# The second half of the swap of the fifth and sixth pairs' inverses: issued by ScalarE in place of SyncE

## The chip, the cores and the metric

The kernel runs on one core of a Trainium2 chip. The metric is the device time of one execution in microseconds; before the change the median of 3 runs is 2953.59 us (2952.55 to 2953.98).

## What is computed

The reference takes 64 graphs of 256 nodes with 512 features each, and one adjacency matrix for all of them. It has two layers, each with a residual and a layer normalisation:

```
# layer 0
mi, mj = x @ Wi.T, x @ Wj.T
x = layernorm(x + deg * (mi + b) + adj @ mj)
# layer 1: attention of 8 heads of 64 channels, masked by the adjacency
q, k, v = x @ Wq.T + bq, x @ Wk.T + bk, x @ Wv.T + bv
attn = softmax(where(adj == 0, -inf, q @ k.T / 8))
x = layernorm(x + (attn @ v) @ Wo.T + bo)
```

The part of interest is the division of the softmax: the products of the exponentials with v are divided by the sums of the exponentials.

## The kernel before

**Groups.** The 64 graphs are worked on in 32 groups of two. A loop (`for g in range(NG - 1)`) runs over the first 31; in one round it does the attention of group g and the first layer of group g + 1. The last group's attention stands behind the loop. All tensors are float32. Most matrix products are made from three parts of each operand (a head rounded down to the fast format, a low part and a "diff"), so each operand of a product is cut by three instructions on three engines: the head by ScalarE, the diff by VectorE (L683), the low part by GpSimd or VectorE (L686).

**Order.** Nearly every instruction is issued through `in_order`, so each engine and each engine's DMA queue runs its instructions as they stand in the code: an instruction that waits holds up all that comes after it on that engine. SyncE does nothing but issue DMAs; ScalarE issues some between its activations.

**Pairs and their division.** The 8 heads of a graph are 4 pairs; the two graphs of a group have 8 pairs, w = 0 to 7 in the code. `scores(g, w)` makes the scores of a pair and returns a step that makes the exponentials: the mask is added by VectorE (L910), the exponential taken by ScalarE (L914), and GpSimd adds two halves (L924). `values(g, w)` multiplies with v into the PSUM tile pav. After each second pair `divide_two` copies pav to the tile aoT (ScalarE, L958) and calls `divide`. That one sums the exponentials on TensorE (den), and its inner step `end` takes the reciprocal on VectorE (L1009) into the first half of the tile spread. The other half of spread gets the same numbers with the two halves of the partitions exchanged: this is the swap, two DMAs from SBUF to SBUF of 64 KB each (L1012). ScalarE sums the inverses for a check (L966). Later `multiply` multiplies aoT by spread on GpSimd (L952), which needs both halves of the swap.

For the last two pairs of a group (w = 7, `last`) the second half of the swap is issued by ScalarE and the sum comes later. For the fifth and sixth pairs (w = 5) `divide_two` is called with `apart=True`, and returns the step `end` so that the loop can place it: it is called `invert` there.

**The loop around the change** (parts left out). The step `invert` stands between the values of the seventh and the eighth pair (L1222); the first line makes the exponentials of the eighth:

```
        later()
        second.neighbours()
        values(g, 6)
        invert()
        fetch_h(b1, 1)
        values(g, 7)
...
        first.give(0)
        multiply()
        second.add(1)
        send_h(b1, 0)
        total_up = divide_two(g, 7)
        split_head(*ao_parts(g, 1, upper))
        go_on()
        split_low(*ao_parts(g, 0, lower), nc.gpsimd)
        own()
        h11 = turn_h(b1, 1)
```

`send_h` (L702) writes rows of the normalised first layer to DRAM, `fetch_h` (L707) reads them back in another order into the tile hB, and `turn_h` transposes hB on VectorE into hF (L517); all these DMAs are issued by SyncE. `give` normalises rows (ScalarE, L509 and L510). The head, low and diff parts of aoT lie in the tiles qT, v and kT at this point. `go_on` and `own` are products of these with Wo on TensorE.

Of the kernel before, what the change touches and what calls it, by code (L numbers as in the profile page):

```python
# [219 lines left out]
def unshifted_path(ctx, tc, flag, x, adj, wiT, wjT, b0, wqT, bq, wkT, bk, wvT, bv, woT, bo, out):  # L220
# [16 lines left out]
    nc = tc.nc  # L237
# [5 lines left out]
    NB = 2  # L243
    NG = B // NB
# [20 lines left out]
    def bank(name):  # L265
        return ps_m.tile([P, 512], F32, tag="mm", name=name)
# [11 lines left out]
    def in_order(ins):  # L278

        tc.keep_in_program_order(ins)  # L280
# [4 lines left out]
    def matmul(*args, **kw):  # L285
        in_order(nc.tensor.matmul(*args, **kw))  # L286
# [41 lines left out]
    rtot = const.tile([P, B, NC // 2], F32, name="rtot")  # L328
# [601 lines left out]
    def target(g, w):  # L930

        i, pr = divmod(w, NC)
        return aoT[g][:, pr // 2 * 2:pr // 2 * 2 + 2, i * N:(i + 1) * N]
# [20 lines left out]
    def divide_two(g, w, apart=False):  # L954

        dst = target(g, w)
        last = w == NB * NC - 1 and g < NG - 1
        in_order(nc.scalar.copy(dst, pavs[g]))  # L958
        i, pr = divmod(w, NC)
        end = divide(dst, [made.pop((g, w - 1))[1], made.pop((g, w))[1]],  # L960
                     rtot[:, NB * g + i, pr // 2:pr // 2 + 1], last, last or g == NG - 1 and w == 3)
        return end if apart else end()

    def total(rden, total_out):
        unused = p1.tile([P, N], F32, tag="unused", name="unused")
        in_order(nc.scalar.activation(unused, rden, AF.Identity, accum_out=total_out))  # L966
# [27 lines left out]
        low = p1.tile([P, 2, N], F32R, tag="xdiff" if g else "hD", name="early")  # L994
        return [both[:, 0], low, both[:, 1]], aoT[g][:, 0:2, :N]

    def divide(dst, pks, total_out, last, other):


        den = bank("den")[:, :N]  # L1000
        for pp in range(2):
            for j in range(2):
                q = 2 * pp + j
                matmul(den[q * R:(q + 1) * R, :], ones[:, :R], pks[pp][:, j, :], start=True, stop=True,
                       tile_position=(0, q * R))
        def end():
            spread = (p3 if other else p1).tile([P, 2, N], F32, tag="mj" if other else "spread", name="spread")
            rden = spread[:, 0, :]
            in_order(nc.vector.reciprocal(rden, den))  # L1009
            for half in range(2):  # L1010
                issuer = nc.scalar if last and half else nc.sync
                in_order(issuer.dma_start(out=spread[half * DH:(half + 1) * DH, 1, :],  # L1012
                                          in_=spread[(1 - half) * DH:(2 - half) * DH, 0, :]))
            products.append((dst, spread))
            if last:
                return lambda: total(rden, total_out)
            total(rden, total_out)

        return end
# [112 lines left out]
    for g in range(NG - 1):  # L1132
# [28 lines left out]
        values(g, 0)  # L1161
        values(g, 1)
        divide_two(g, 1)
        run([scores(g, 2), scores(g, 3)])
        load_xB(b3)
# [15 lines left out]
        early = cut_early(g)  # L1181
        split_head(*early)
        divide_two(g, 3)
        now, later = scores(g, 4), scores(g, 5)
        now()
# [21 lines left out]
        if g == 0:  # L1207
            add_output_bias(0)
            add_output_bias(1)
        first.stat(0)  # L1210
        invert = divide_two(g, 5, True)
        now, later = scores(g, 6), scores(g, 7)
        aoP[g] = three(("qT", "kT"))
# [88 lines left out]
    g = NG - 1  # L1302
# [18 lines left out]
    last = NB * NC - 1  # L1321
# [70 lines left out]
```

## Time and profile before

| | |
|---|---|
| median of 3 runs | 2953.59 us |
| profiled execution | 2951.97 us |
| its span, first to last instruction | 2950.1 us |
| TensorE matmul busy | 2878.1 us, 98% |
| VectorE busy | 2265.1 us, 77% |
| GpSimd busy | 1482.3 us, 50% |
| ScalarE busy | 1309.4 us, 44% |
| swap DMAs issued by SyncE | 223 |
| swap DMAs issued by ScalarE | 31 |
| mean granted TensorE clock | 0.999 |

The profile is of one execution. Lines such as L1012 are lines of the kernel; most matmuls are recorded under the line of one helper (L286) and told apart by their tiles. Names such as PE, DVE, ACT, POOL and SP stand for TensorE, VectorE, ScalarE, GpSimd and SyncE; a q behind the name (SPq) means the engine's sequencer, which issues DMAs. A timeline has the start in us from the span's beginning, the length, the instruction with its output and inputs, and in brackets the idle time ahead of it and what ended it. A wait list gives total us, times, and the longest. The chain that ended last is followed back from the last instruction, at each step to what released it. One round of the loop takes some 90 to 91 us.

### The profile page before, as it was taken

The numbers are of one execution on the slowest core, as the hardware profiler recorded it, in microseconds if no ns is written. First come the engines' busy times: TensorE is split into PE (matmuls) and PEld (weight loads), VectorE is DVE, ScalarE is ACT, GpSimd is POOL, SyncE is SP. The second block draws the span as 40 slices with busy tenths as digits, with TensorE's granted clock in tenths as the row PEclk, the third lists the DMA queues.
The fourth block names the chain that finished last, engine by engine and source line by source line (L and its number), as shares of the span: only waits on it lengthen the run. The fifth ranks groups of instructions, "written<-read, shape, count | busy, mean of one in ns | idle before, by whom it ended". The sixth has DMA issues, their size and how long they took to land.

```text
span 2950.1 us, 45509 instructions
## 1 busy us (share of the span) xinstructions
PE 2878.1 (98%) x16902; PEld 2140.1 (73%) x16902; DVE 2265.1 (77%) x3275; ACT 1309.4 (44%) x2412; POOL 1482.3 (50%) x1049
## 2 busy tenths in 40 slices
PE   9999999999999999999999999999999999999998
PEld 6577777777777777777777777777777777777775
DVE  5777787777877778877778777787777787777875
ACT  4444444444444444444444444444444444444443
POOL 3555555454555455454545544555545555454553
PEclk9999999999999999999999999999999999999999
DMA  7577766777666776667776677766677766777653
GB/s 251 194 258 239 247 218 218 255 245 266 217 219 239 266 247 230 212 226 264 242 247 222 221 249 252 268 212 215 238 267 240 246 214 215 257 248 261 213 211 116
DMA packets 303345, 690.54 MB, mean 234 GB/s; under 512 B 25744, under 2 KB 171280, under 8 KB 302864
## 3 DMA queue, kind: packets, MB, share of 16 engines
q1 hardware_dynamic: 282784, 588.02, 58.4%
q10 hardware_dynamic: 20336, 99.56, 9.5%
q8 instruction: 136, 2.23, 0.3%
q14 instruction: 89, 0.73, 0.1%
HBM read 589.04 MB, written 81.79 MB: 227 GB/s over the span
## 4 chain that ended last, share of the span: by engine, by line
PE 77%; DVE 15%; POOL 3%; DMA 3%; issue 1%; SPq 1%; ACT 1%; POOLq 0%; DVEq 0%; ACTq 0%
PE px L286 26%; PE pxy L286 20%; PE py L286 13%; PE ps L286 7%; PE pav L286 5%; PE pa L286 3%; DVE hF L517 2%; DMA hB<-h_cols 2%; DVE kT L683 2%; DVE spread L1009 2%; DVE st L496 2%; PE po L286 2%; DVE xh L833 1%; PE den L286 1%; DVE xh L830 1%
## 5 line engine op out<-in xcount | busy, mean ns | idle before, releaser
L924 POOL TENSOR_TENSOR pk<-pe 128x512 f32<-128x512 f32 x256 | 347.4, 1368 | 729.5 <-ACT pe L914 729.5
L914 ACT ACTIVATE pe<-pe 128x1024 f32<-128x1024 f32 x256 | 271.0, 1059 | 176.9 <-DVE pe L910 176.9
L504 POOL TENSOR_TENSOR rstd<-ve,mhalf 128x1 f32<-128x1 f32 x256 | 167.5, 654 | 343.4 <-DVE below L502 313.2
L910 DVE TENSOR_TENSOR pe<-ps,maskT 128x1024 f32<-128x1024 f32 x256 | 297.2, 1200 | 3.6 <-PE ps L286 3.6
L1009 DVE RECIPROCAL spread<-den 128x256 f32<-128x256 f32 x127 | 222.7, 1754 | 81.7 <-ACT aoT L958 51.8
L686 POOL TENSOR_TENSOR hL<-hF,hA 128x512 fp32r<-128x512 f32 x93 | 166.4, 1789 | 229.1 <-ACT hA L680 229.1
L774 DVE TENSOR_TENSOR kT<-py,kT 128x512 f32<-128x512 f32 x128 | 88.5, 692 | 226.2 <-ACT kT L773 226.2
L286 PE MATMUL ps<-qT,kT 64*128 64x256 f32 x2048 | 256.6, 390 | 0.0
L286 PE MATMUL pav<-pe,v_sb 128*32 128x256 f32 x4096 | 248.4, 382 | 3.5 <-DVE kT L774 1.5
L286 PEld LDWEIGHTS ps<-qT,kT 64*128 64x128 f32 x2048 | 187.3, 187 | 68.6 <-PE pav L286 26.3
L510 ACT ACTIVATE xh<-xh,shift,rstd 128x512 f32<-128x512 f32 x256 | 208.8, 816 | 8.6
L286 PEld LDWEIGHTS pav<-pe,v_sb 128*32 128x32 f32 x4096 | 120.0, 110 | 116.8 <-issue 24.4
L680 ACT ACTIVATE hA<-hF 128x512 fp32r<-128x512 f32 x124 | 78.3, 632 | 278.5 <-DVE hF L517 255.5
L286 PE MATMUL px<-factor,x_head 128*128 128x512 f32 x720 | 200.2, 400 | 0.0
L286 PE MATMUL py<-factor,x_diff 128*128 128x512 f32 x720 | 192.8, 390 | 2.0 <-ACT kT L773 2.0
L368 POOL TENSOR_TENSOR xh<-xh,degb 128x1024 f32<-128x1024 f32 x64 | 182.5, 2853 | 22.8 <-ACT degb L365 20.9
L286 PE MATMUL px<-factor,x_low 128*128 128x512 f32 x720 | 192.8, 390 | 0.0
L952 POOL TENSOR_TENSOR aoT<-aoT,spread 128x512 f32<-128x512 f32 x127 | 165.9, 1306 | 41.6 <-DMA spread<-spread 35.4
L686 POOL TENSOR_TENSOR x_low<-xT,x_head 128x1024 fp32r<-128x1024 f32 x60 | 144.2, 2403 | 67.6 <-ACT x_head L680 64.7
L286 PE MATMUL py<-hD,factor 128*128 128x512 f32 x640 | 175.9, 397 | 2.2 <-ACT kT L773 2.2
L286 PE MATMUL px<-hA,factor 128*128 128x512 f32 x640 | 175.7, 397 | 0.0
L496 DVE BATCH_NORM_STATS2 st<-xh 128x6 f32<-128x512 f32 x256 | 174.3, 681 | 0.2
(160 smaller groups left out, 6809.1 us busy)
## 6 DMA issues: line engine op xcount, KB each, us to landing
factor<-wi SPq DMA_DIRECT2D x120, 768.0 KB, 8.7
factor<-wo SPq DMA_DIRECT2D x120, 768.0 KB, 6.2
factor<-wv SPq DMA_DIRECT2D x93, 768.0 KB, 7.8
factor<-wk SPq DMA_DIRECT2D x93, 768.0 KB, 7.0
factor<-wq ACTq DMA_DIRECT2D x62, 768.0 KB, 7.6
factor<-wq SPq DMA_DIRECT2D x62, 768.0 KB, 7.4
xB<-in_x_dram SPq DMA_DIRECT2D x256, 128.0 KB, 4.1
xh<-in_x_dram SPq DMA_DIRECT2D x64, 512.0 KB, 3.9
```

The costliest lines, as they stand in the source:

```text
L286: in_order(nc.tensor.matmul(*args, **kw))
L368: in_order(nc.gpsimd.tensor_tensor(xh[b], xh[b], degb, ALU.add))
L496: order(nc.vector.bn_stats(st, t))
L504: order(nc.gpsimd.tensor_tensor(rstd, ve, mhalf, ALU.pow))
L510: order(nc.scalar.activation(t, t, AF.Identity, bias=shift, scale=rstd))
L686: in_order(engine.tensor_tensor(parts[1], src, parts[0].bitcast(F32), ALU.subtract))
L774: in_order(nc.vector.tensor_add(dst, Y, dst))
L910: in_order(nc.vector.tensor_add(pe.rearrange("p j t q -> p j (t q)"), ps.rearrange("p j t q -> p j (t q)"), maskT.rearrange("p t q -> p (t ...
L914: in_order(nc.scalar.activation(flat, flat, AF.Exp, scale=QSCALE, accum_out=etot[:, NB * g + i, pr:pr + 1]))
L924: in_order(nc.gpsimd.tensor_tensor(pk, pe[:, :, 0, :], pe[:, :, 1, :], ALU.add))
L952: in_order(nc.gpsimd.tensor_tensor(d, d, spread, ALU.mult))
L1009: in_order(nc.vector.reciprocal(rden, den))
```

## The change

The condition for ScalarE as issuer of the second half gets wider: beside the last pairs of a group in the loop it now takes every call with `apart=True`, which is the one for the fifth and sixth pairs (31 calls). `divide` gets this as a parameter of its own, `urgent`; what else hangs on `last` (where the sum is made, which pool spread comes from) stays as it is.

```diff
-                     rtot[:, NB * g + i, pr // 2:pr // 2 + 1], last, last or g == NG - 1 and w == 3)
+                     rtot[:, NB * g + i, pr // 2:pr // 2 + 1], last, last or g == NG - 1 and w == 3, last or apart)
...
-    def divide(dst, pks, total_out, last, other):
+    def divide(dst, pks, total_out, last, other, urgent):
...
             for half in range(2):
-                issuer = nc.scalar if last and half else nc.sync
+                issuer = nc.scalar if urgent and half else nc.sync
                 in_order(issuer.dma_start(out=spread[half * DH:(half + 1) * DH, 1, :],
                                           in_=spread[(1 - half) * DH:(2 - half) * DH, 0, :]))
```

## The prediction

> **What bounds the kernel now.** I read the first part of the page and the summary of the chain that ended last, then the chain itself across one group, then the timelines of the engines in the same 20 us, and last the list of waits.
>
> ```profile
> PE 2878.1 (98%) x16902; PEld 2140.1 (73%) x16902; DVE 2265.1 (77%) x3275; ACT 1309.4 (44%) x2412; POOL 1482.3 (50%) x1049
> PE 77%; DVE 15%; POOL 3%; DMA 3%; issue 1%; SPq 1%; ACT 1%; POOLq 0%; DVEq 0%; ACTq 0%
> ```
>
> TensorE is busy nearly throughout, yet the chain leaves it for a fifth of the span: VectorE, DMA and SyncE's queue hold pieces of the path. The chain in the group around 1316 us shows where:
>
> ```profile
> 1314.44 1.67 DVE spread L1009
> 1316.11 0.02 issue
> 1316.13 0.47 SPq L1012
> 1316.60 0.05 issue
> 1316.65 0.59 SPq L1012
> ...
> 1317.34 3.10 DMA hB<-h_cols
> 1320.43 0.02 issue
> 1320.46 1.13 DVE hF L517
> ...
> 1329.88 0.70 DVE xh L833
> 1330.59 0.04 issue
> 1330.63 0.97 PE pxy L286 x3
> ```
>
> Columns are start, length, what. The reciprocal of the fifth and sixth pairs (L1009) ends at 1316.11; SyncE issues both halves of the swap; only then can it issue the fetch of the turned h (hB, L707, at 1317.34); that lands at 1320.43 and VectorE transposes it into hF. From there VectorE works without a gap until TensorE is released at 1330.63. So the swap's second issue is on the path not for its data but because the fetch stands behind it in SyncE's queue.
>
> What else could hold VectorE at that point is its own next reciprocal, that of the seventh and eighth pairs:
>
> ```profile
> 1318.64 1.76 DVE L1009 RECIPROCAL spread<-den 128x256 f32<-128x256 f32 x1 [0.80 <-PE den L286]
> 1320.46 1.13 DVE L517 STREAM_TRANSPOSE hF<-hB 128x512 f32<-128x512 f32 x1
> ```
>
> It ends at 1320.40, only 0.06 before the transpose. In the timelines of the groups at 1679 and 2131 us, where the fetch came sooner, the transpose starts 4.21 us after the fifth and sixth pairs' reciprocal ended; that is the floor that the other reciprocal sets. I measured this start in groups 1 to 30 of the 31: mean 4.50, median 4.38, worst 5.58 us. From it to the next group's first reciprocal takes 59.25 us, within 0.1 us in 27 of the 29 groups where it can be measured, and from that first reciprocal to the fifth and sixth pairs' takes 26.75 us always. So every group's length follows that start one for one, down to 4.21.
>
> [...] for the seventh and eighth pairs both queues issue at 1320.43 (0.47 and 0.50 us), and over the run ScalarE's halves land 2.2 us after issue, SyncE's 2.1. [...] behind another swap the issue takes 0.59 instead of 0.47, the fetch right behind the swaps 0.53 against 0.35 for its line's median; the simultaneous pair shows no lengthening, but its ScalarE half lands 0.29 us later than SyncE's (1322.66 against 1322.37). [...] here swaps of 64 KB land 1.9 us or more after issue[...].
>
> **The change, part by part.** It touches 31 swaps, one in each group of the loop; the last group takes the other call and stays.
>
> 1. Removed from SyncE: one issue per group, 0.59 us and the 0.05 before it, 0.64 in all. The next in the queue is the fetch: 1317.34 becomes 1316.70. The fetch's data was sent at 1312.68 and is long there. [...] the fetch loses up to the 0.29 seen above. So the landing moves by 0.35 to 0.64 us; I take 0.5.
>
> 2. What this is worth. Each group gains the smaller of that shift and its distance from 4.21. The distances in the 30 groups are 1.37, 1.16, 0.67, 0.64, 0.50, 0.46, 0.45, 0.33, 0.32, 2 x 0.24, 2 x 0.23, 0.19, 2 x 0.17, 0.16, 2 x 0.15, 2 x 0.14, 0.11, 0.10, 0.09, 2 x 0.08, 0.05, 0.03, 2 x 0. Group 0, where the other reciprocal ends late, gains nothing. With a shift of 0.35 the sum is 5.9 us, with 0.5 it is 6.8, with 0.64 it is 7.4. More shift would bring little, because VectorE's reciprocal is late next.
>
> 3. Added to ScalarE: one issue, 0.50 us (the row of the other swap), in front of the sum of the inverses. It waits for the same reciprocal as that sum, so the wait is not new. Behind it stand these:
>
> ```profile
> 1316.14 0.42 ACT L966 ACTIVATE unused<-spread 128x256 f32<-128x256 f32 x1
> ...
> 1316.87 0.81 ACT L510 ACTIVATE xh<-xh,shift,rstd 128x512 f32<-128x512 f32 x1
> 1318.21 0.58 ACT L958 COPY aoT<-pav 128x512 f32<-128x512 f32 x1 [0.53 <-PE pav L286]
> 1320.43 0.50 ACTq L1012 DMA_DIRECT2D spread<-spread  x1
> ```
>
> They slip by 0.5 us, the idle 0.53 ahead of the copy takes that up, and a further 1.6 us lies idle between the copy and the next issue at 1320.43. The normalised rows (L510) leave for DRAM through SyncE some 0.3 us later (1317.96 before), their fetch starts 0.3 us later than 1321.17 and lands near 1324.2 instead of 1323.89, and VectorE takes it at 1327.46: 3 us of cover. Cost 0. Without this cover it would be 0.5 us a group, 15 us in all.
>
> 4. The second half's own landing: before 1316.65 + 2.0 = 1318.65; after, 1316.13 + 2.23 = 1318.36, so 0.29 us earlier. GpSimd's multiply waits for it, and behind the multiply stands the low part v, for which TensorE waits:
>
> ```profile
> 1318.81 1.30 POOL L952 TENSOR_TENSOR aoT<-aoT,spread 128x512 f32<-128x512 f32 x1 [1.02 <-DMA spread<-spread]
> 1320.06 1.29 POOL L686 TENSOR_TENSOR v<-aoT,qT 128x512 fp32r<-128x512 f32 x1
> ```
>
> TensorE's gap there (0.34 us) will shrink to about 0.05, but it then reaches earlier the next two operands that VectorE makes (py<-kT at 1323.86 and 1327.59). In two groups the landing came so late that TensorE stood 1.7 and 1.9 us (the groups at 1044 and 591 us), and both lengths still fit 59.25 plus the start; in a third, at 1497 us, it stood 2.04 us and the group was 0.56 us longer. So this wait costs from about 1.9 us on, and I count 0.
>
> The sum is -6.8 us: 2951.97 for the profiled execution becomes 2945.2, and from the median of the runs, 1.62 above it, 2953.6 becomes **2946.8 us**. The measurement of this kernel can tell about 0.2%, or 5.9 us, from no change.
>
> **The rivals.**
>
> A, the forecast, chance 0.66: with its two bounds and 1.5 us of scatter between runs it gives 2944.7 to 2949.2. In 0.56 the gain passes 5.9 us, in 0.10 it falls short of it [...].
>
> B, no change, 0.17: the fetch is issued earlier but lands where it did[...]. For it speaks the 0.53 of the fetch behind the swaps; against it that the fetch takes 3.10 us to land here and 3.0 in the median of its line, so it hardly queues. Time 2953.6.
>
> C, more gain, 0.10: TensorE's wait for v is on the path too, and the 0.29 us of point 4 counts in all 31 groups: 9 us more, 2938. For it speaks this row of the waits (the first below), against it the two groups that stood 1.7 and 1.9 us and lost nothing.
>
> D, slower, 0.07: ScalarE's issue is held before it starts. [...] SyncE shows it for weight loads (second row):
>
> ```profile
> PE px L286 <- POOL v L686: 19.9, 31, 2.0
> SPq L456 <- DMA factor<-wq: 29.3, 26, 2.8
> ```
>
> On ScalarE such a wait holds up the copy and the next swap. Up to 0.53 + 1.64 = 2.2 us are covered; at the 2.8 us of this row, with the issue's 0.5, each group loses 1.1 us, 31 groups 34, less the 6.8: 2981. Against it: SyncE's second half starts 0.05 us after the first in every group, so nothing holds it today.
>
> **How the numbers follow.** Faster: 0.56 + 0.10 of A and C = 0.66. Same: 0.10 + 0.17 = 0.27. Slower: 0.07. The range of 2940 to 2953.6 leaves out D, half of B and half of C, 0.2 together.
>
> **What would show it.** Right: the fetch L707 issued about 0.6 us after the reciprocal's end instead of 1.23; SyncE's and the second half's issues side by side as for the other swap; hF at 4.21 us after the reciprocal in nearly every group, ending VectorE's waits for hB (5.4 us, 11 times); the chain going from L1009 of the seventh and eighth pairs, over TensorE's den, straight to hF; the ScalarE copy still at 2.1 us. Wrong: hF at 4.4 with the fetch early (B), groups shorter than 90.1 us (C), or ScalarE's L958 after 2.2 us and its issue starting late (D).

## The result, and the profile after

The changed kernel takes 2945.02 us (median of 9 runs, 2943.75 to 2948.21); the kernel before, in the same comparison, 2953.10 us (9 runs). The ratio is 0.9975 with a 95% interval of 0.9966 to 0.9983, so the gain is 8.1 us, between 5.0 and 10.0. The profiled execution of the changed kernel took 2945.87 us, its span is 2944.0 us, 6.1 less than before.

The first part of the page and the summary of the chain, after:

```profile
PE 2877.9 (98%) x16902; PEld 2136.6 (73%) x16902; DVE 2261.4 (77%) x3275; ACT 1306.6 (44%) x2412; POOL 1482.4 (50%) x1049
PE 81%; DVE 14%; POOL 1%; DMA 1%; issue 1%; ACT 1%; SPq 0%; POOLq 0%; DVEq 0%; ACTq 0%
```

The engines do what they did. In the chain, DMA has gone from 3% to 1%, GpSimd from 3% to 1% and SyncE's queue from 1% to nothing, and TensorE's share has grown from 77% to 81%. The chain in the group around 1314 us, the same group as was shown of before:

```profile
1314.72 1.86 PE pav L286 x32
1316.59 0.48 PE den L286 x8
1317.06 0.02 issue
1317.09 1.76 DVE spread L1009
1318.84 0.96 DVE hF L517
...
1328.08 0.70 DVE xh L833
1328.78 0.04 issue
1328.83 0.98 PE pxy L286 x3
```

The piece from the fifth and sixth pairs' reciprocal over SyncE's two issues and the fetch is gone. The chain now comes from TensorE's sums over the reciprocal of the seventh and eighth pairs straight to the transpose into hF, as the prediction asked for. SyncE's queue and ScalarE's timeline in that group (the fifth and sixth pairs' reciprocal ends at 1314.55):

```profile
1314.57 0.47 SPq L1012 DMA_DIRECT2D spread<-spread  x1
1315.13 0.54 SPq L707 DMA_DIRECT2D hB<-h_cols  x1
```

```profile
1314.58 0.50 ACTq L1012 DMA_DIRECT2D spread<-spread  x1
1315.12 0.42 ACT L966 ACTIVATE unused<-spread 128x256 f32<-128x256 f32 x1 [0.62 <-DVE kT L683]
...
1315.85 0.81 ACT L510 ACTIVATE xh<-xh,shift,rstd 128x512 f32<-128x512 f32 x1
1316.65 0.58 ACT L958 COPY aoT<-pav 128x512 f32<-128x512 f32 x1
1318.88 0.50 ACTq L1012 DMA_DIRECT2D spread<-spread  x1
```

The two halves leave side by side, the fetch 0.6 us after the reciprocal instead of 1.23. ScalarE's sum and normalisation slip by 0.5 us, and the copy L958 starts without the idle 0.53 us it had, 2.1 us after the reciprocal as before.

Not all groups got there. These are VectorE's lines in the group that begins its swap at 591 us:

```profile
593.61 1.76 DVE L1009 RECIPROCAL spread<-den 128x256 f32<-128x256 f32 x1 [0.80 <-PE den L286]
596.57 1.12 DVE L517 STREAM_TRANSPOSE hF<-hB 128x512 f32<-128x512 f32 x1 [1.19 <-DMA hB<-h_cols]
```

The fetch took 4.9 us from issue to landing there (in an ordinary group 2.9), and this is what the DMA view of 591.2 to 597 us shows (queue, packets, MB and share; then issue, size and us to landing):

```profile
q8 instruction: 1, 0.02, 1.9%
...
hB<-h_cols SPq DMA_DIRECT2D x1, 256.0 KB, 4.9
```

One packet of q8, the queue that the view puts down as instruction, went through while the fetch was under way (0.02 MB; 1.9% of 16 engines in the view's 5.8 us, which is 1.8 us of one engine). All five groups in which hF starts later than 4.25 us (at 591, 1044, 1495, 1586 and 2488 us) have such a packet in flight with the fetch. So have five groups that are on time; of the 20 groups without one, the latest fetch landed at 4.04 us after the reciprocal. The times at which the packets began differ: in four of the late groups it was 2.0 to 2.5 us after the reciprocal, in the fifth (at 1586 us) it began at 0.61 and the fetch's issue itself took 1.61 us instead of 0.54; in the five groups on time it began at 1.0 or earlier, or at 3.1. This is a coincidence in time; that the packet held up the fetch wasn't tested by a run of its own. In the list of waits after:

```profile
PE px L286 <- POOL v L686: 5.0, 8, 1.2
...
DVE hF L517 <- DMA hB<-h_cols: 4.5, 6, 1.2
```

TensorE's wait for v has shrunk from 19.9 us in 31 groups to 5.0 us in 8, and VectorE's for hB from 11 times to 6, yet only from 5.4 us to 4.5: the many short waits are gone, the few long ones stayed.

### The profile page after: what moved, and what is told of

Read it like the earlier page. It is cut to its first block, busy times and chain, and to the rows that moved or that the text cites. A ratio compares the mean times of both kernels' runs of the same rounds, so it can differ in the third digit from the quotient of the medians.

```text
span 2944.0 us, 45539 instructions
## 1 busy us (share of the span) xinstructions
PE 2877.9 (98%) x16902; PEld 2136.6 (73%) x16902; DVE 2261.4 (77%) x3275; ACT 1306.6 (44%) x2412; POOL 1482.4 (50%) x1049
## 3 DMA queue, kind: packets, MB, share of 16 engines
q8 instruction: 136, 2.23, 0.3%
## 4 chain that ended last, share of the span: by engine, by line
PE 81%; DVE 14%; POOL 1%; DMA 1%; issue 1%; ACT 1%; SPq 0%; POOLq 0%; DVEq 0%; ACTq 0%
PE px L286 26%; PE pxy L286 20%; PE py L286 13%; PE ps L286 8%; PE pav L286 7%; PE pa L286 4%; DVE hF L517 2%; DVE kT L683 2%; DVE spread L1009 2%; PE den L286 2%; PE po L286 2%; DVE st L496 2%; DVE xh L833 1%; DVE xh L830 1%; DMA hB<-h_cols 1%
## 5 line engine op out<-in xcount | busy, mean ns | idle before, releaser
L680 ACT ACTIVATE hA<-hF 128x512 fp32r<-128x512 f32 x124 | 78.0, 629 | 278.9 <-DVE hF L517 274.4
```

## The experiments

Two theories stood against each other. The **queue theory**, that of the prediction: the change pays because the fetch no longer stands behind the second half's issue in SyncE's queue. The **landing theory**: it pays because the second half of the swap lands earlier (at 2.23 us after the reciprocal in the median, before 2.56), so that GpSimd's multiply and the low part v behind it come earlier. "Groups" below are groups 1 to 30, and times in them count from the end of the fifth and sixth pairs' reciprocal.

### Fetch first, both halves still by SyncE

```diff
 # the kernel before
-        invert()
         fetch_h(b1, 1)
+        invert()
```

> The kernel before with one change: the fetch of h (L707) stands ahead of the swap in SyncE's queue; SyncE still issues both halves. Queue theory (the change pays because the fetch no longer stands behind the second half's issue): the fetch is issued before the reciprocal ends, hF starts at the 4.2 us floor in all groups, and the time falls at least as far as with the change: by 8 to 10 us, to 2943 to 2945. Landing theory (the change pays because the second half lands earlier and GpSimd's multiply starts sooner): both halves land as before or later, so no gain, 2953.

Measured: 2945.16 us, ratio 0.9972 (0.9962 to 0.9983). SyncE's queue and VectorE in the group whose reciprocal ends at 1315.36:

```profile
1314.44 0.33 SPq L707 DMA_DIRECT2D hB<-h_cols  x1
1315.38 1.11 SPq L1012 DMA_DIRECT2D spread<-spread  x2
```

```profile
1317.89 1.76 DVE L1009 RECIPROCAL spread<-den 128x256 f32<-128x256 f32 x1 [0.81 <-PE den L286]
1319.57 1.04 DVE L517 STREAM_TRANSPOSE hF<-hB 128x512 f32<-128x512 f32 x1
```

The fetch leaves before the swap, and the transpose follows the reciprocal directly, in every group (4.21 us). The second half lands at 2.63, a little later than before the change, and TensorE waits for v in all 31 groups, 24.3 us in sum. The whole gain is there without ScalarE and without an earlier half. This speaks for the queue theory and against the landing theory.

The starts of hF alone would have paid for more (8.5 us in sum over groups 1 to 29, and 0.1 us a group behind them). In five groups with an instruction packet the second half, not the fetch, now landed late, 3.9 to 4.8 us after the reciprocal, and the second hF of these groups came 0.3 to 1.1 us late. In the other 25 groups the half landed anywhere between 2.5 and 3.6 us, and the second hF started at 11.11 to 11.14 us in all of them. So the landing of the half, within these bounds, isn't on the path at all; only one that is later still costs time, and more on this stands below.

### A spare issue in the fetch's place

```diff
 # the changed kernel; idle_issue: a DMA of 64 KB from aoT to DRAM, by SyncE
         invert()
+        idle_issue(g)
         fetch_h(b1, 1)
```

> The changed kernel plus one spare DMA of 64 KB that SyncE issues between the first half of the swap and the fetch, so that the fetch is issued about as late as in the kernel before, while the second half still leaves by ScalarE at once. Queue theory: the gain goes, 2952 to 2954, the fetch at about 1.2 us after the reciprocal and hF back near 4.4. Landing theory: the gain stays, 2945.

Measured: 2946.47 us, ratio 0.9981 (0.9973 to 0.9988). My expectation failed, though the trace says why: the fetch was issued at 1.23 us as wanted, but it landed 2.86 us later, at 4.09, where it had landed 3.13 us after issue, at 4.36, before the change. So hF still started at the floor, at 4.22 in the median, and the gain stayed. SyncE's queue and VectorE in the group whose reciprocal ends at 1313.44:

```profile
1313.98 0.59 SPq L1026 DMA_DIRECT2D spare<-aoT  x1
1314.67 0.53 SPq L707 DMA_DIRECT2D hB<-h_cols  x1
```

```profile
1317.65 1.11 DVE L517 STREAM_TRANSPOSE hF<-hB 128x512 f32<-128x512 f32 x1
```

The run doesn't tell the theories apart, but it narrows the queue theory: the 0.64 us of earlier issue aren't needed for most of the gain. A fetch issued as late as before the change, which lands a quarter of a microsecond sooner after its issue, is early enough in most groups. What counts is when the fetch lands. I made the delay larger:

```diff
         invert()
+        idle_issue(g, 0)
+        idle_issue(g, 1)
         fetch_h(b1, 1)
```

> The changed kernel with two spare DMAs of 64 KB issued by SyncE between the first half of the swap and the fetch, so that the fetch is issued at about 1.8 us after the reciprocal, later than in the kernel before, while the second half still lands at 2.25. Queue theory: hF starts near 4.65 in every group, 0.43 us past the floor, so the changed kernel's gain is lost and more: 2945 plus 31 groups by 0.43, 2957 to 2960. Landing theory: the gain stays, 2945.

Measured: 2974.11 us, ratio 1.0071 (1.0057 to 1.0085), slower than before the change although the second half landed at 2.24. VectorE in the group whose reciprocal ends at 1325.90:

```profile
1328.44 1.76 DVE L1009 RECIPROCAL spread<-den 128x256 f32<-128x256 f32 x1 [0.80 <-PE den L286]
1330.73 1.15 DVE L517 STREAM_TRANSPOSE hF<-hB 128x512 f32<-128x512 f32 x1 [0.53 <-DMA hB<-h_cols]
```

The transpose waits for hB in each group. Its mean start is 5.15 us instead of 4.36 in the changed kernel; 0.79 us by 31 groups is 24.5 us of the 29 us measured. Some 3 us more come from behind it: the second hF starts 7.01 us after the first again, against 6.90 in the changed kernel. The expected 2957 to 2960 was too low because the fetch landed 3.2 us after its issue, not 2.9. Here only the fetch is late, and the gain is lost: this is the queue theory's mechanism run backwards.

### Holding ScalarE longer

```diff
 # the changed kernel, in end()
             products.append((dst, spread))
+            if urgent and not last:
+                in_order(nc.scalar.dma_start(out=spare, in_=spread[DH:P, 0, :]))
```

> The changed kernel with a spare DMA of 64 KB issued by ScalarE right behind the second half: ScalarE is held for another 0.5 us at the place where the change holds it. If that hold is covered, as the prediction has it (2.2 us), the time stays at 2944 to 2947, with the copy of pav (L958) at about 2.6 us instead of 2.1. If ScalarE's hold is on the path, 0.5 us in each of 31 groups, 2960.

Measured: 2944.97 us, ratio 0.9974 (0.9963 to 0.9986), the changed kernel's time.

```profile
1314.96 0.50 ACTq L1012 DMA_DIRECT2D spread<-spread  x1
1315.50 0.84 ACTq L1016 DMA_DIRECT2D spare<-spread  x1
...
1317.84 0.57 ACT L958 COPY aoT<-pav 128x512 f32<-128x512 f32 x1
```

The spare issue took 0.84 us rather than 0.5, and the copy came 2.91 us after the reciprocal (1314.93 here). Nothing waited for it. So the 0.5 us that the change puts on ScalarE is free with at least 0.8 us to spare.

### How late may the second half land?

```diff
 # the kernel before: a function given to end() is called between the halves
+                if between and not half:
+                    between()
 ...
-        invert = divide_two(g, 5, True)
+        invert = divide_two(g, 5, True, lambda: fetch_h(b1, 1))
 ...
         invert()
-        fetch_h(b1, 1)
```

> The kernel before with the fetch issued by SyncE between the two halves of the swap; ScalarE issues nothing new. The fetch leaves about when it does with the change, the second half about 0.6 us later than in the kernel before. Queue theory: the gain of the change, 2944 to 2947; TensorE's wait for v grows to about 0.9 us a group and costs nothing. Landing theory: slower than before by up to 0.6 us a group, 2953 to 2971.

Measured: 2962.63 us, ratio 1.0032 (1.0020 to 1.0044): slower, the landing theory's side. The second half landed not 0.6 us later but 1.5 us (at 4.04), 2.9 us after its issue. The 256 KB of the fetch, issued 0.59 us before it, were under way with it; whether that is the reason, no run isolates. The queue theory isn't refuted by this, since hF started at 4.22 in the median, but my claim that a longer wait for v costs nothing is. The other run with a late half agrees:

```diff
 # the changed kernel: end() issues half 0 only and returns the issue of half 1
         first.give(0)
+        second_half()
         multiply()
```

> The changed kernel with the second half issued by ScalarE later, behind the normalisation of a row block (L510), so that the fetch leaves early as with the change and the second half lands about 3.7 us after the reciprocal, 1.2 us later than before the change. TensorE's wait for v grows to about 1.5 us a group. Queue theory with my estimate that this wait is free up to about 1.9 us: the gain stays, 2945 to 2948. Landing theory: each us that the half lands later than before is lost, 31 groups by 1.2 us, up to 2990.

Measured: 2965.55 us, ratio 1.0046 (1.0032 to 1.0059). ScalarE issued the half at 0.92 us, ahead of the end of the activations that stand before it in its queue, and it landed at 4.16. Where does a half that lands at 4.1 us cost? GpSimd, VectorE and TensorE of the run with the fetch between the halves, in the group whose reciprocal ends at 1321.12:

```profile
1326.48 1.26 POOL L686 TENSOR_TENSOR v<-aoT,qT 128x512 fp32r<-128x512 f32 x1
```

```profile
1327.28 1.01 DVE L686 TENSOR_TENSOR v<-aoT,qT 128x512 fp32r<-128x512 f32 x1
```

```profile
1327.80 0.73 PE L286 MATMUL px<-factor,v 128*128 128x512 f32 x2 [1.72 <-POOL v L686]
```

VectorE's own low part (of other columns) takes 1.01 us here; in the profile of the changed kernel it takes 0.68 in the mean of 31. It starts as early as there (6.16 us after the reciprocal; in the changed kernel's group at 1315 us 6.17), but there GpSimd's v had ended 1.29 us before, and here it is still under way for 0.46 us. It ends 0.55 us after GpSimd's v, at 1328.29, and about that much after it in the other late groups as well (7.68 and 8.22, 6.51 and 7.06). Why it is longer there, no run isolates. VectorE's chain is later by this: the low part ends at 7.26 us instead of 6.86 in the median, and the second hF of the group starts at 11.52 us instead of 11.11. In sum over the 30 groups the second hF comes 12.3 us later than in the changed kernel. TensorE's clock falls as well. These are windows of 2 us of the group at 1594 us, in which TensorE waited 2.2 us for v (columns: window, length, busy us of PE, PEld, DVE, ACT, POOL, then granted clock, DMA share, GB/s):

```profile
1599.00:1601.00 2.00, 0.00 (x0) 0.00 (x0) 1.80 (x6) 1.11 (x2) 2.00 (x2) 1.00 0.68 182
1601.00:1603.00 2.00, 1.86 (x5) 1.48 (x6) 1.97 (x4) 0.94 (x3) 2.00 (x3) 0.58 0.05 18
1603.00:1605.00 2.00, 2.00 (x7) 1.57 (x6) 1.93 (x6) 1.77 (x4) 1.77 (x3) 0.57 0.42 122
1605.00:1607.00 2.00, 2.00 (x11) 1.62 (x10) 2.00 (x3) 0.07 (x1) 2.00 (x2) 1.00 0.52 139
```

After the idle stretch the granted clock is 0.58 and 0.57 in two windows, then 1.00 again, and the rest of the group is 0.45 us longer. Over the span the granted clock is 0.994, where the changed kernel has 0.999; TensorE's waits for v come to 59.5 us in 31 groups, the longest 2.8.

The group at 1497 us of the kernel before shows the same: TensorE waited 2.04 us for v, to 1503.88, and these are its windows from 1502 us on:

```profile
1502.00:1504.00 2.00, 0.12 (x1) 0.13 (x2) 1.93 (x6) 1.15 (x2) 2.00 (x3) 1.00 0.63 149
1504.00:1506.00 2.00, 2.00 (x6) 1.54 (x7) 1.93 (x7) 1.11 (x2) 2.00 (x2) 0.66 0.13 48
1506.00:1508.00 2.00, 2.00 (x6) 1.60 (x5) 1.97 (x4) 1.63 (x3) 1.77 (x3) 0.50 0.50 135
1508.00:1510.00 2.00, 2.00 (x10) 1.60 (x10) 2.00 (x3) 0.23 (x1) 1.86 (x2) 0.99 0.69 165
```

The clock was granted at 0.50 for 3.41 us, from 1504.63 to 1508.04, and the group was 0.56 us longer. After the waits of 1.94 us at 591 us and of 1.74 us at 1044 us of the same profile it stayed at 1.00. What parts the waits with a slower clock behind them from those without isn't shown by these lengths. How often it happened in the run with the fetch between the halves is an estimate from the mean clocks: 0.005 of 2960.7 us is 14.8 us, a stretch of 3.41 us at 0.50 takes 1.7 of it, and with the rounding of the clocks that makes seven to ten such stretches more than in the changed kernel; at 0.45 us each they hold 3 to 5 us.

To part the two branches I moved v ahead of the multiply, so that TensorE doesn't wait for it:

```diff
 # the kernel with the fetch between the halves
         first.give(0)
+        split_low(*ao_parts(g, 0, lower), nc.gpsimd)
         multiply()
 ...
-        split_low(*ao_parts(g, 0, lower), nc.gpsimd)
         own()
```

> The kernel with the fetch between the halves (2962.6 us), with GpSimd's low part v, for which TensorE waits, moved ahead of the multiply that waits for the swap. The late second half then reaches the end only by the head that ScalarE takes of the multiplied aoT and by what VectorE makes of it. If both branches cost there (the head's branch 0.41 us a group by the start of the second hF, TensorE's wait for v the rest, 0.23), it ends at 2954 to 2957. If all the cost was TensorE's wait for v, it falls to 2945; if all was the head's branch, it stays at 2962.

Measured: 2958.47 us, ratio 1.0018 (1.0009 to 1.0027), 4 us less than with v behind. Its runs lie far apart, 2951.6 to 2962.8, and the profile is of the fastest; there TensorE's wait for v is zero and VectorE's low part ends at 6.88 us instead of 7.27. So part of the cost went with v, but how much each branch holds is not settled by it. In this profile there is a step: in the seven groups whose half landed at 4.21 us or later the second hF starts at 12.1 us or later, in the others at 11.24 at the latest. What makes the step stays open.

### Better versions

```diff
 # the changed kernel
-        invert()
         fetch_h(b1, 1)
+        invert()
```

> The changed kernel with the fetch moved ahead of the swap in SyncE's queue as well. Queue theory: in most groups hF already starts at the floor of 4.21, so little is left; the five groups of the profile in which the fetch came late (4.3 us beyond the floor in sum) get to the floor, 2941 to 2943. Landing theory: no difference to the changed kernel, 2945.

Measured: 2941.24 us, ratio 0.9959 (0.9945 to 0.9972). hF starts at the floor in all groups, also where a packet of q8 goes through, as the fetch lands at 1.9 us in the median and 2.3 us of delay are covered. The 3.8 us below the changed kernel are near what its five late groups had left over the floor, 4.3 us; two groups here, in which the swap was complete only at 4.42 and 3.77 us, lost 0.9 us of it again.

> The changed kernel with the fetch ahead of the swap (2941.2 us) and v ahead of the multiply. TensorE's wait for v, 0.53 us a group in that profile, goes away. If that wait is free there, as VectorE's chain is later, the time stays at 2940 to 2942; if it is on the path, it falls by up to 16 us, to 2925.

The edit moves v ahead of the multiply, as above, in the kernel with the fetch first. Measured: 2939.89 us, ratio 0.9954 (0.9940 to 0.9968). TensorE's mean wait for v went from 0.53 us to 0, and at most 1.4 us of 16 came back, which the intervals don't part from nothing: at ordinary landings that wait is free.

```diff
 # the changed kernel with the fetch first
+        h11 = turn_h(b1, 1)
         total_up = divide_two(g, 7)
 ...
-        h11 = turn_h(b1, 1)
```

> The changed kernel with the fetch ahead of the swap and with VectorE's transpose of hB moved ahead of the reciprocal of the seventh and eighth pairs, into the 0.80 us in which VectorE waits there for TensorE. It leaves out nothing. If that reciprocal is the next bound, as the floor of 4.21 says, the work behind it (1.1 us of transpose) shrinks and only some 0.8 us of it comes back as a later reciprocal: up to 0.35 us a group faster, 2932 to 2942. If the floor is something else, no gain, 2942 to 2945, or a loss by the later swap of these pairs.

Measured: 2940.03 us, ratio 0.9955 (0.9941 to 0.9969). An ordinary group gets shorter (its second hF starts at 10.93 us in the median instead of 11.12 with the fetch first alone), but where the fetch lands late it now holds up the reciprocal as well, and the mean hardly moves, 11.13 instead of 11.15. The floor can be lowered by 0.2 us; nearly all of it is lost again to the late groups.

## Why the prediction was right, point by point

**The bound and the mechanism** were as stated: the fetch behind the swap in SyncE's queue, the group's length following hF's start, and the reciprocal of the seventh and eighth pairs as the next bound at 4.21 us. Moving the fetch alone gives the gain. Issuing it 0.64 us later alone doesn't take it away, because it lands sooner after its issue than before the change; issuing it 1.2 us later does.

**The size**: 6.8 us were forecast, 8.1 (5.0 to 10.0) measured. Two terms of the sum were mis-sized and nearly cancel. The shift of the landing was taken as 0.5 us with bounds of 0.35 to 0.64; it was 0.88 in the median (4.36 to 3.48). The issue moved by 0.64 as worked out, but the fetch also landed 2.89 us after issue instead of 3.13: the 0.29 us taken off for ScalarE's half beside it was an estimate from one simultaneous pair and doesn't show in the landing, and a quarter of a microsecond came on top. Why, was not tested; with SyncE's second half beside it the fetch needs 3.13 (half ahead of it) and 3.26 us (half behind it), with ScalarE's 2.89. With a shift of 0.88 the same sum is 7.9 us. But in five groups with an instruction packet in flight, which the prediction didn't reckon with, the fetch gained little or came later, and hF's starts in groups 1 to 29 fell by 4.2 us in sum, not 7.9.

Second, the time behind hF's start was taken as fixed; it shrank by 0.11 us a group, 3.2 us in all, most of it in one place: the second hF starts 6.90 instead of 7.01 us after the first where the first starts at the floor (the two groups at the floor before the change, at 1679 and 2131 us, with 6.97 and 6.90, showed that already, and I overlooked it). Together that is 7.4 us in groups 1 to 29 of the profiles. So the mechanism was forecast, but that 6.8 came so near to 7.4 is in part luck. The start-up before these groups was 1.4 us longer in the profile after, so its span fell by 6.1. That isn't the change's doing as far as the traces show: the profile after has a granted clock of 0.50 from 72.86 to 76.27 us, in the start-up, and the profile before has 1.00 there.

**ScalarE's cost of 0**: right, and covered by 0.8 us more at least. The rows left for DRAM 0.3 us later, as worked out.

**The second half's landing**, 0.29 us earlier: measured 0.33, and TensorE's gap went to 0.00 in most groups. For the ordinary groups counting it at 0 was right: in the run with the fetch first, landings from 2.5 to 3.6 us all gave the same second hF. What I put beside it, that this wait costs only from about 1.9 us on, was wrong as a rule: halves that land at 4.1 us, with waits of 1.6 to 2.1 us in most groups, cost 17 us or more against the changed kernel, 12.3 us of it on VectorE's chain, where the low part took 1.01 us beside GpSimd's v, and by the estimate above 3 to 5 us by the slower clock. The group at 1497 us lost its 0.56 us with the clock at 0.50 behind a wait of 2.04 us; behind the wait of 1.94 us at 591 us the clock was 1.00. Two such waits don't show a limit of 1.9 us; that was my estimate.

**The rivals**: B (no earlier landing) and C (more gain by v) didn't occur, and D's wait on ScalarE neither: its issue starts 0.03 us after the reciprocal. The sign given for C, groups shorter than 90.1 us, did appear (an ordinary group now takes 90.04 to 90.13), but the time was gained between the first and the second hF, on VectorE, and not on TensorE's wait: without that wait at most 1.4 us came back.

## What to carry to other kernels

Ask of each DMA issue not only who waits for its data, but what stands behind it in its queue: here a fetch on the path stood behind a transfer that was not, and landed 0.88 us later for it, 0.64 us by the issue and the rest in flight; over the run that cost 8 us. Before an issue is moved to another engine, try the order: putting the urgent fetch first gave the same gain with no engine changed. And a gain by an earlier transfer ends where the next producer is late, so measure that floor first, in the groups where the transfer happened to come early.

## What the runs showed of the hardware

- The profiles before and after list 136 packets of 16 KB on q8, the queue put down as instruction. A packet took 0.9 to 1.8 us in the profile after, and hF started 0.5 to 1.3 us past the floor in five of the ten groups where one was in flight with the fetch.
- TensorE's granted clock was 0.50 for 3.41 us behind a wait of 2.04 us in the kernel before (1504.63 to 1508.04), and 0.58 and 0.57 in two windows of 2 us behind a wait of 2.2 us with the fetch between the halves. Behind waits of 1.94 and 1.74 us in the kernel before it was 1.00.
- DMAs that ScalarE issued went out ahead of the end of activations queued before them: with the late half at 0.92 us, where the normalisation before it ended near 1.6; in the profile after the load L456 at 148.33 us, where the activation L680, begun at 148.26, ended at 148.89.
- A 64 KB half of the swap issued 0.6 us behind the 256 KB fetch on the same queue took 2.9 us to land in the run with the fetch between the halves; behind the other half of the swap, in the kernel before, 2.0.
